# A routed expert layer whose weights are loaded once an expert, with the down products by Strassen's scheme

## The chip, the cores and the metric

The kernel is one program on one core of a Trainium2 chip. Its time is the device time of one execution in microseconds; the figure given is the median of three executions. The core has a matmul engine (PE, whose weight loads are listed apart as PEld), a vector engine (DVE), a scalar engine (ACT), a general engine (POOL), and a queue engine (SP) that starts transfers. Each of them takes its own instructions in order, and semaphores hold one behind another.

## The reference

Two layers over x of 2 x 2048 x 256, all in float32. Layer 0 is a gated linear attention and a quantised product; layer 1 is a 16-head attention with ALiBi bias and, beside it, a mixture of eight experts. Only the last is touched by the change:

```python
# xf: 4096 x 256; W_gate, W_up: 8 x 1024 x 256; W_down: 8 x 256 x 1024; TOP_K = 2
logits = xf @ gate_W.T
pi = _sinkhorn(-logits)                       # 20 rounds
_, top_idx = jax.lax.top_k(pi, TOP_K)
g = jnp.einsum('nd,efd->enf', xf, W_gate)
u = jnp.einsum('nd,efd->enf', xf, W_up)
y = jnp.einsum('enf,edf->end', jax.nn.silu(g) * u, W_down)
out = jnp.zeros_like(xf)
for k in range(TOP_K):
    out = out + y[top_idx[:, k], n_ar] * pi[:, k:k + 1]
```

Each token goes to two of eight experts, so there are 8192 rows in all. The routing worked out from the reference's inputs gives the experts 1047, 977, 950, 1003, 1054, 1044, 1029 and 1088 rows.

## The kernel before

The program runs layer 0, then the attention of layer 1 in "units" (one pass of the loop in `attention`: score matmuls L1823, exponentials L1832, weighted sums L1846), and in the gaps of those units the routing on DVE. The routing writes each row's token number and weights into a table in DRAM by 64 scatters (`sends`, L2222). When the units end, `Experts.run` (L2582) goes through the experts' rows.

**Blocks.** Rows are cut into full blocks of 256 (`BS`) and small ones of 32. An expert with `count` rows has `(count + 127) >> 8` full blocks; what is left goes into small blocks, four of which make a `Group`. The usual way handles 32 full blocks (`FULLS`) and two groups. The flags `c.special`, `c.more` and `c.general` say whether more blocks, or the whole general way (`general_way`, which computes everything again by other means), must be run after it.

**One block.** `load` gathers the expert's gate and up weights (2 MB, `load_gate_up`) by an indirect transfer from POOL (L2255), and reads the block's 256 table rows on SP (`load_places`, L2271); `load_down` gathers the down weights (1 MB) likewise; `fetch_rows` gathers the 256 tokens. `combine(u)` forms the sums of weights that Strassen's scheme (in Winograd's form: 7 products in place of 8) needs, four DVE operations of 128 x 512 for each half u of the hidden features; it overwrites the up weights with one of them. `open_rows` transposes the tokens on PE and forms their sums.

**The hidden products.** `hidden` (L2329) makes, for each u, seven products of four 128 x 128 x 128 matmuls. Their results go to three PSUM banks w, z and v, and ACT and DVE take partial results out between them. The order is h1 (to w), h2 (z), h6 (w), h5 (v), h7 (w), h4 (w), h3 (v). The last DVE operation of a half is `two *= sg[:, 1]`, behind the last SiLU.

**The down products.** `add_rows` (L2371) is a generator that `hidden` of the next block steps through by `next(others)`: once after h2, once after h5 and twice after h7, in each u, so eight times a block. Each step makes two matmuls of 128 x 128 x 256 (`multiply`); there are sixteen for a block, plain, into one bank `y_ps` with both row tiles side by side. At the end two DVE operations of 128 x 256 scale the sums (`send`, L2402) and two indirect transfers add them to the output. The last block's are made `apart`, each tile in a bank of its own.

`InOrder` keeps the expert phase's PE, DVE and ACT instructions in the order in which the program states them. So the place of a DVE operation in the program is its place in DVE's queue. PE takes matmuls in order too. In the traces one float32 matmul is two records.

**The order of one pass of the loop** in `run` is: `load` of block n+2; the generator of block n-1's down products; `hidden` of block n with, inside it, `combine(1)` of block n (u = 0, after the first step of the generator) and `combine(0)` of block n+1 (u = 1), `fetch_rows` of n+2 and `open_rows` of n+1; then `load_down` of n+2, and a step of a group if one is due.

Of the kernel before, what the change touches and what calls it, by code (L numbers as in the profile page):

```python
# [64 lines left out]
P = 128  # L65
# [3 lines left out]
ST = 512  # L69
# [23 lines left out]
NBLK = NFULL + NSMALL  # L93
ROWS = NFULL * BS + NSMALL * SB
FULLS, GROUPS = 2 * B * N // BS, 2
SPARE = B * N
RW = NE + 1
SINKHORN_ITERS = 20
# [1604 lines left out]
def attention(  # L1703
# [41 lines left out]
    def decide():  # L1745
        yield from routing.blocks(p2)

        high = p2.tile([P, 1], F32, tag="high", name="high")
        vector.tensor_reduce(high, norms[:, 0, :], AX.X, ALU.max)
        small = p2.tile([P, 1], F32, tag="small", name="small")  # L1750
        inside = p2.tile([P, NSTRIP * HG * 8], F32, tag="sk_part", name="inside", bufs=1)
        vector.tensor_scalar(
            inside, spans.rearrange("p s h n j -> p (s h n j)"), math.exp(-SPAN), None, ALU.is_ge
        )
        vector.tensor_reduce(small, inside, AX.X, ALU.min)
        yield
        least = p2.tile([P, 1], F32, tag="least", name="least")
        entry = p2.tile([P, NT, NE], F32, tag="sk_ex", name="entry")
        vector.tensor_tensor(entry, routing.second, pi, ALU.mult)
        yield  # L1760
        of_token = p2.tile([P, NT], F32, tag="sk_r", name="of_token")
        vector.tensor_reduce(of_token, entry, AX.X, ALU.max)
        vector.tensor_reduce(least, of_token, AX.X, ALU.min)
        yield
        within = p2.tile([P, 1], F32, tag="within", name="within")
        vector.tensor_scalar(within, least, TINY, None, ALU.is_ge)
        vector.tensor_tensor(within, within, small, ALU.mult)
        vector.tensor_scalar(least, grown, GROWTH, None, ALU.is_le)
        vector.tensor_tensor(within, within, least, ALU.mult)
        yield  # L1770
        yield
        ps = ps_m.tile([1, P + 1], F32, tag="mm", name="d_ps")
        nc.tensor.matmul(ps[:, 0:P], lhsT=high, rhs=ident, start=True, stop=True)
        nc.tensor.matmul(
            ps[:, P : P + 1], lhsT=within, rhs=c.ones_mat[:, 0:1], start=True, stop=True
        )
        yield
        row = p2.tile([1, P + 1], F32, tag="drow", name="drow")
        vector.tensor_copy(row, ps)
        both = p2.tile([1, P // 2], F32, tag="dboth", name="dboth")  # L1780
        vector.tensor_tensor(both, row[:, 0 : P // 2], row[:, P // 2 : P], ALU.mult)
        vector.tensor_scalar(both, both, 0.98 * LIMIT**2, None, ALU.is_le)
        ok = p2.tile([1, 1], F32, tag="dok", name="dok")
        vector.tensor_reduce(ok, both, AX.X, ALU.min)
        vector.tensor_scalar(row[:, P : P + 1], row[:, P : P + 1], float(P), None, ALU.is_equal)
        vector.tensor_tensor(ok, ok, row[:, P : P + 1], ALU.mult)
        vector.tensor_scalar(ok, ok, -1.0, 1.0, ALU.mult, ALU.add)
        vector.tensor_copy(c.general, ok)
        vector.tensor_tensor(ok, ok, routing.over[:, 0:1], ALU.max)
        vector.tensor_copy(c.special, ok)  # L1790
        yield
# [101 lines left out]
    def rooms(name, n, shape, dt=F32):  # L1893
# [8 lines left out]
        if name == "group_s":  # L1902
            return p2.tile(shape, F32, tag="sk_equal", name=name, bufs=1)
        if name == "wgateup":
            return operands.heads[(0, 1, 3)[n % 3]].rearrange("p j t -> p (j t)")
        if name == "wdown" and n % 3 < 2:
            return operands.heads[2][:, n % 3, :]
        if name in ("hT", "wdown"):
            room = large("pt", 2 if name == "wdown" else n % 2)
            return room if name == "wdown" else room.rearrange("p (f r) -> p f r", f=NFC)  # L1910
        early = operands.first_values.rearrange("p t d -> p (t d)")
        late = other_values.rearrange("p t d -> p (t d)")
        rest = partial(large, "pt", 3)
# [25 lines left out]
        return p2.tile(shape, dt, tag=name, name=name, bufs=5)  # L1939

    bias = value_bias()
    experts = Experts(tc, a, out, c, rooms, range(FULLS), range(GROUPS))
    ahead = experts.todo[0:2]
    for n, (pieces, widths, masks, ended) in enumerate(units):
        if n in (len(units) // 4 - 4, len(units) // 4):
            next(bias)
        if n == len(units) - BEGIN:
            for left in (background, decision, sends):
                for _ in left:
                    pass  # L1950
            for block in ahead:
                block.load_places()
            for block in ahead:
                block.load_gate_up()
        if n == len(units) - FETCH:
            for block in ahead:
                block.fetch_rows()
        if len(units) - FETCH < n <= len(units) - FETCH + 4:
            ahead[0].combine(0, range(n - len(units) + FETCH - 1, n - len(units) + FETCH))
        pt = scores(pieces, widths)  # L1960
        calm = not unmasked or len(unmasked[1]) <= CALM
        if unmasked:
            keep_only(*unmasked)
        unmasked = pt, masks
        before = len(chores)
        waiting.append((pieces, pt, ended))
        if len(waiting) > LATE:
            add_up()
        if before and chores:
            do_chore()  # L1970
        if routed:
            for _ in range(1 + n % 2):
                next(sends, None)
            if calm:
                next(decision, None)
        elif calm:
            routed = next(background, True) is True
        if n == len(units) - 4:
            ahead[0].open_rows()
    keep_only(*unmasked)  # L1980
    while waiting:
        add_up()
    for block in ahead:
        block.load_down()

    def rest():
        while chores:
# [6 lines left out]
class Routing:  # L1994
# [3 lines left out]
    def __init__(self, tc, vector, pool, a, c, group):  # L1998
# [15 lines left out]
        self.first, self.second = (  # L2014
            pool.tile([P, NT, NE], F32, tag=name, name=name) for name in ("first", "second")
        )
        self.over = pool.tile([1, 2], F32, tag="over", name="over")
        self.places = [
            pool.tile([P, NT], I32, tag=name, name=name) for name in ("place0", "place1")
        ]  # L2020
# [5 lines left out]
    def steps(self, pool, psum, pi):  # L2026
# [119 lines left out]
        for to, mark in zip(self.places, (first, second)):  # L2146
# [4 lines left out]

            vector.tensor_scalar(to, at, float(ROWS - 1), None, ALU.min)
            yield
        self.end = end

    def blocks(self, pool):

# [43 lines left out]
        for n in range(2):  # L2201
# [3 lines left out]
            )  # L2205
            vector.tensor_copy(self.c.wpart[:, n, :], part)
        over = self.over
        for n, done in enumerate((FULLS, 4 * GROUPS)):
            vector.tensor_scalar(
                over[:, n : n + 1], end[0:1, n, NE - 1 :], float(done), None, ALU.is_gt  # L2210
            )
# [31 lines left out]
class Block:  # L2243
# [156 lines left out]
    def send(self, c, ps, y, group=None):  # L2400
        e = self.e
        e.nc.vector.scalar_tensor_tensor(  # L2402
            y[:, c, :], ps, self.wt[:, c : c + 1], e.c.half_bias, ALU.mult, ALU.add
        )
        send = e.nc.gpsimd.indirect_dma_start(  # L2405
            out=e.out, in_=y[:, c, :], in_offset=None,
            out_offset=bass.IndirectOffsetOnAxis(ap=self.to[:, c : c + 1], axis=0),
            compute_op=ALU.add,
        ).ins


        if group and c:
            e.tc.declare_no_dep(send, group=group, reason="no row is in two of a block's tiles")
        if group:
            e.tc.add_to_no_dep_group(group, send)
            if e.latest:
                e.tc.add_manual_dep(
                    send, e.latest,
                    mybir.DependencyInfo(mybir.DependencyClass.Sync, mybir.DependencyReason.DATA),
                    reason="the same row may be in another block",  # L2420
                )
        else:
            e.latest = send.name


class Group:
# [121 lines left out]
class Experts:  # L2548

    def __init__(self, tc, a, out, c, rooms, blocks, groups):
        self.tc, self.nc, self.a, self.out, self.c = tc, tc.nc, a, out, c
# [1 line left out]
            InOrder(tc, engine) for engine in (self.nc.tensor, self.nc.vector, self.nc.scalar)  # L2555
        )
        self.rooms, self.latest = rooms, None
        self.todo = [Block(self, n, b) for n, b in enumerate(blocks)]
        self.between = deque()
        at = 3  # L2560
        for g in groups:
# [20 lines left out]
    def run(self, begun=None):  # L2582
# [12 lines left out]
        for n, block in enumerate(todo):  # L2595
            if n + 2 < len(todo):
                todo[n + 2].load()
            last = n + 1 == len(todo)
            others = todo[n - 1].add_rows() if n else begun or iter(())
            if last:  # L2600
                others = self.closing(others, block)
            meanwhile = (
                partial(block.combine, 1), (lambda: None) if last else partial(todo[n + 1].combine, 0)
            )
            for part, _ in enumerate(block.hidden(others, meanwhile)):
                if part == 1 and n + 2 < len(todo):
                    todo[n + 2].fetch_rows()
                if part == 2 and not last:
                    todo[n + 1].open_rows()
            for _ in others:  # L2610
                pass
            if n + 2 < len(todo):
                todo[n + 2].load_down()
            while between and between[0][0] <= n and not last:
                between.popleft()[1]()
        for _, step in between:
            step()

    def closing(self, others, block):

        while next(others, others) is None:
            next(others, None)
            yield
        yield from block.add_rows(apart=True)


def layer1_experts(tc, a, out, c, blocks, groups):
# [181 lines left out]
```

## Time and profile before

| what | value |
|---|---|
| median of three executions | 1504.07 us (1503.86 to 1504.57) |
| the profiled execution's own time | 1507.06 us |
| its span, first to last instruction | 1504.8 us |
| PE busy | 1444.7 us (96%) |
| DVE busy | 1009.7 us (67%) |
| ACT busy | 730.3 us (49%) |
| POOL busy | 538.4 us (36%) |
| moved by transfers | 191.94 MB |
| first hidden product of block 0 | 827.72 us from the span's start |
| last DVE scaling of the last block | begins at 1492.46 us |

In a timeline line the columns are: start, duration, engine, source line, operation, what it writes and reads, shapes, count, and in brackets how long the engine was idle before it and on whom it waited. Line L121 is the helper that keeps the order, so most operations of the expert phase carry it; the tile names tell them apart. Rooms are shared with attention, so `qk` holds weights there, `larger` and `va` hold hidden values and results. `h_ps` are the hidden banks, `y_ps` the down bank, `x_ps` the transposes of tokens, `o_ps` the attention's sums and `o_sb` their copies. A "wait" row gives an engine's total time behind another.

### The profile page before, as it was taken

The numbers are of one execution on the slowest core, as the hardware profiler recorded it, in microseconds if no ns is written. First come the engines' busy times: TensorE is split into PE (matmuls) and PEld (weight loads), VectorE is DVE, ScalarE is ACT, GpSimd is POOL, SyncE is SP. The second block draws the span as 40 slices with busy tenths as digits, with TensorE's granted clock in tenths as the row PEclk, the third lists the DMA queues.
The fourth block names the chain that finished last, engine by engine and source line by source line (L and its number), as shares of the span: only waits on it lengthen the run. The fifth ranks groups of instructions, "written<-read, shape, count | busy, mean of one in ns | idle before, by whom it ended". The sixth has DMA issues, their size and how long they took to land.

```text
span 1504.8 us, 33474 instructions
## 1 busy us (share of the span) xinstructions
PE 1444.7 (96%) x13712; PEld 1180.6 (78%) x13712; DVE 1009.7 (67%) x2567; ACT 730.3 (49%) x1557; POOL 538.4 (36%) x449
## 2 busy tenths in 40 slices
PE   7879999999989999999999999999999999999996
PEld 4656767676757777777666899989899998989995
DVE  6788677565448888874445767667666776666663
ACT  4444554555367888888876332333232332323231
POOL 4342222121120000399961234343434544343432
PEclk9999999999989999999999999999999999999998
DMA  8001010410353120420034656575766867576531
GB/s 236 0 15 59 30 57 30 120 58 29 81 151 60 31 62 25 95 35 5 5 131 157 224 195 199 191 286 175 261 198 218 252 210 254 193 253 241 174 83 23
DMA packets 75986, 191.94 MB, mean 128 GB/s; under 512 B 19136, under 2 KB 56768, under 8 KB 63360
## 3 DMA queue, kind: packets, MB, share of 16 engines
q0 software_dynamic: 28256, 144.23, 28.8%
q1 hardware_dynamic: 46464, 44.30, 11.9%
q8 instruction: 110, 1.80, 0.5%
q10 hardware_dynamic: 1104, 1.18, 0.3%
q14 instruction: 52, 0.43, 0.1%
HBM read 157.95 MB, written 32.10 MB: 126 GB/s over the span
## 4 chain that ended last, share of the span: by engine, by line
PE 56%; DVE 2%; ACT 1%; issue 1%; POOL 0%; POOLq 0%; another core or an unknown queue 0%
PE h_ps L121 26%; PE y_ps L121 15%; PE sc L1823 6%; PE o_ps L1846 5%; PE f_ps L1544 1%; PE h_ps L2491 1%; PE x_ps L121 1%; DVE pt L121 1%; ACT pt L1832 1%; PE h_ps L2526 0%; DVE o_sb L121 0%; ACT larger L121 0%; DVE onT L121 0%; DVE on L121 0%; DVE larger L121 0%
## 5 line engine op out<-in xcount | busy, mean ns | idle before, releaser
L1832 ACT ACTIVATE pt<-sc 128x512 f32<-128x512 f32 (+5 forms) x746 | 312.4, 517 | 78.2 <-issue 39.2
L1823 PE MATMUL sc<-qk 32*128 32x256 f32 (+3 forms) x3022 | 208.1, 361 | 3.6 <-ACT pt L1832 1.6
L121 DVE TENSOR_TENSOR larger<-larger,h_ps 128x512 f32<-128x512 f32 x160 | 109.9, 687 | 144.3 <-ACT larger L121 79.0
L1823 PEld LDWEIGHTS sc<-qk 32*128 32x128 f32 x3022 | 158.9, 189 | 46.1 <-ACT pt L1832 25.3
L121 PE MATMUL y_ps<-qk,larger 128*128 128x256 f32 x704 | 173.4, 380 | 0.3 <-DVE larger L121 0.3
L1846 PE MATMUL o_ps<-pt,va 128*32 128x256 f32 (+3 forms) x3022 | 166.2, 341 | 3.2 <-DVE o_sb L121 1.9
L121 ACT COPY larger<-h_ps 128x512 f32<-128x512 f32 x128 | 74.5, 582 | 172.7 <-PE h_ps L121 168.2
L121 DVE TENSOR_TENSOR pt<-pt,keepmask 128x128 f32<-128x128 f32 x512 | 117.4, 283 | 48.0 <-ACT pt L1832 46.9
L2405 POOL DMA_INDIRECT out<-va,to x64 | 102.7, 1604 | 124.3 <-DVE larger L121 49.1
L1846 PEld LDWEIGHTS o_ps<-pt,va 128*32 128x32 f32 x3022 | 103.3, 111 | 51.0 <-issue 20.8
L2222 POOL DMA_INDIRECT table<-rows,place x64 | 68.2, 1066 | 194.1 <-DVE pt L121 181.7
L121 PEld LDWEIGHTS y_ps<-qk,larger 128*128 128x128 f32 x704 | 123.9, 191 | 12.3 <-DVE larger L121 0.7
L121 PEld LDWEIGHTS h_ps<-va,qk 128*128 128x128 f32 x1024 | 126.6, 192 | 7.6 <-ACT larger L121 2.3
L121 PE MATMUL h_ps<-va,qk 128*128 128x128 f32 x1024 | 130.6, 276 | 1.9 <-ACT larger L121 1.9
L2568 POOL DMA_INDIRECT xb<-normed,to x64 | 65.5, 1024 | 140.5 <-DVE by L2291 71.8
L121 ACT ACTIVATE larger<-larger 128x512 f32<-128x512 f32 x64 | 40.4, 632 | 117.8 <-DVE larger L121 117.8
L121 ACT ACTIVATE va<-va 128x512 f32<-128x512 f32 x64 | 40.4, 632 | 100.2 <-DVE va L121 96.3
L121 PE MATMUL y_ps<-larger 128*128 128x256 f32 x320 | 79.0, 380 | 0.0
L121 POOL TENSOR_TENSOR pause<-ones_mat,expo 128x4 f32<-128x4 f32 x64 | 68.6, 1072 | 2.0
L121 ACT COPY va<-h_ps 128x512 f32<-128x512 f32 x64 | 36.9, 577 | 56.4 <-PE h_ps L121 51.1
L121 PE MATMUL h_ps<-larger,qk 128*128 128x128 f32 x512 | 62.7, 276 | 0.0
L121 PEld LDWEIGHTS h_ps<-larger,qk 128*128 128x128 f32 x512 | 59.7, 192 | 2.1 <-issue 2.1
(318 smaller groups left out, 2798.5 us busy)
## 6 DMA issues: line engine op xcount, KB each, us to landing
qk<-qk SPq DMA_DIRECT2D x32, 256.0 KB
qk<-qk SPq DMA_DIRECT2D x64, 128.0 KB
va<-v SPq DMA_DIRECT2D x4, 1208.0 KB
v<-v SPq DMA_DIRECT2D x8, 574.0 KB
normed<-xn SPq DMA_DIRECT2D x8, 512.0 KB
out<-acc SPq DMA_DIRECT2D x16, 256.0 KB
acc<-in_x SPq DMA_DIRECT2D x7, 512.0 KB
table<-rows,place POOLq DMA_INDIRECT x64
```

Of the source, the lines that this page charges most:

```text
L121: return lambda *a, **k: self.tc.keep_in_program_order(begin(*a, **k))
L1544: multiply(out[r : r + HR], left[:, r : r + HR], *args, **how)
L1823: nc.tensor.matmul(scs[r][:, at : at + q1 - q0], lhsT=heads[rows, 1, kb * P : (kb + 1) * P], rhs=heads[rows, 0, qt * QT + q0 : qt * QT + q ...
L1832: nc.scalar.activation(pt[:, r, part], scs[r][:, part], AF.Exp)
L1846: nc.tensor.matmul(sums[bank][r * HR : (r + 1) * HR, to + q0 : to + q1], lhsT=values[b, way][:, kb, h * VC : h * VC + HR], rhs=pt[:, r, at ...
L2222: send = self.tc.keep_in_program_order(self.nc.gpsimd.indirect_dma_start(out=self.c.table, in_=self.rows[:, t, :], in_offset=None, out_off ...
L2405: send = e.nc.gpsimd.indirect_dma_start(out=e.out, in_=y[:, c, :], in_offset=None, out_offset=bass.IndirectOffsetOnAxis(ap=self.to[:, c : ...
L2491: self.e.nc.tensor.matmul(ps[rows, :], lhsT=self.xT[:, c * P + r * SB : c * P + (r + 1) * SB], rhs=self.w[:, r, at : at + ST], start=c == ...
L2568: self.nc.gpsimd.indirect_dma_start(out=to, out_offset=None, in_=self.c.normed, in_offset=bass.IndirectOffsetOnAxis(ap=at, axis=0),)
```

## The change

The usual way now requires that each expert has exactly four full blocks (`OWN = FULLS // NE`): a third entry of `over` is 1 where that holds, and the flag for the general way is set where it doesn't. An `Expert` object loads its weights once by plain transfers on SP: gate and up in eight pieces of 256 KB (four for each u), down in one of 1 MB, two experts' worth of room each. `combine` runs once an expert. A new `turn_down` forms four sums of the down weights once an expert, and a new `sums` forms four sums of the hidden values once a block, behind `hidden`. `add_rows` makes seven products of four 128 x 128 x 128 matmuls in seven steps; their results lie in three quarters w, z, v of the one bank `y_ps`, and seven DVE operations of 128 x 128 (`put`) take them out. The last block's down products stay plain and apart.

```diff
+        vector.tensor_tensor(ok, ok, routing.over[:, 2:3], ALU.mult)
         vector.tensor_scalar(ok, ok, -1.0, 1.0, ALU.mult, ALU.add)
         vector.tensor_copy(c.general, ok)
...
+        own = tile_("own_blocks", [1, NE])
+        vector.tensor_scalar(own, self.full[0:1, :], float(OWN), None, ALU.is_equal)
+        vector.tensor_reduce(over[:, 2:3], own, AX.X, ALU.min)
...
         if name == "wgateup":
-            return operands.heads[(0, 1, 3)[n % 3]].rearrange("p j t -> p (j t)")
+            return operands.heads[n % 2].rearrange("p j t -> p (j t)")
+        if name == "wdown":
+            return operands.heads[2][:, n % 2, :]
...
-    experts = Experts(tc, a, out, c, rooms, range(FULLS), range(GROUPS))
+    experts = OwnExperts(tc, a, out, c, rooms, range(FULLS), range(GROUPS))
...
+        if n == len(units) - FETCH - 4:
             for block in ahead:
                 block.load_places()
-            for block in ahead:
-                block.load_gate_up()
+        if 0 <= n - len(units) + BEGIN < 8:
+            u, part = divmod(n - len(units) + BEGIN, 4)
+            experts.experts[0].load_gate_up(u, range(part, part + 1))
...
-    for block in ahead:
-        block.load_down()
+    experts.experts[0].load_down()
...
+class Expert:
+    def load_gate_up(self, u, parts=range(4)):
+        if not u:
+            self.w = self.e.rooms("wgateup", self.k, [P, 4 * FF])
+            self.wgu = self.w.rearrange("p (j c f) -> p j c f", j=2, c=2)
+        rows = self.e.a["wgateup"][self.k * P : (self.k + 1) * P, :]
+        for n in parts:
+            at = slice(n * FF + u * ST, n * FF + (u + 1) * ST)
+            self.e.tc.keep_in_program_order(
+                self.e.nc.sync.dma_start(out=self.w[:, at], in_=rows[:, at])
+            )
...
+    def turn_down(self):
...
+        vector.tensor_tensor(t1, b12, b11, ALU.subtract)
+        vector.tensor_tensor(t2, b22, t1, ALU.subtract)
+        vector.tensor_tensor(t3, b22, b12, ALU.subtract)
+        vector.tensor_tensor(t4, b21, t2, ALU.subtract)
+        self.parts = (b11, b21, b22, t4, t1, t2, t3)
...
+class OwnBlock(Block):
...
+    def sums(self):
...
+        vector.tensor_tensor(s1, a21, a22, ALU.add)
+        vector.tensor_tensor(s2, s1, a11, ALU.subtract)
+        vector.tensor_tensor(s3, a11, a21, ALU.subtract)
+        vector.tensor_tensor(s4, a12, s2, ALU.subtract)
+        self.parts = (a11, a12, s4, a22, s1, s2, s3)
+
+    def add_rows(self, apart=False):
+        if apart:
+            yield from super().add_rows(True)
+            return
+        e = self.e
+        y = e.rooms("y", self.n, [P, NC, E])
+        ps = e.rooms("y_ps", self.n, [P, ST])
+        w, z, v = (ps[:, n * P : (n + 1) * P] for n in range(3))
...
+        def product(n, to, first=False, last=False):
+            for f in range(4):
+                e.tensor.matmul(
+                    to, lhsT=self.parts[n - 1][:, f, :], rhs=self.expert.parts[n - 1][:, f, :],
+                    start=first and f == 0, stop=last and f == 3, skip_group_check=True,
+                )
+
+        def put(c, half, src, more):
+            e.vector.scalar_tensor_tensor(
+                y[:, c, half], src, self.wt[:, c : c + 1], more[:, half], ALU.mult, ALU.add
+            )
...
+        product(1, w, first=True)
+        put(0, left, w, bias)
+        yield
+        product(2, z, last=True)
+        put(0, left, z, y[:, 0, :])
+        yield
+        product(6, w)
+        put(0, right, w, bias)
+        yield
+        product(5, v)
+        yield
+        product(7, w)
+        put(1, right, w, bias)
+        put(1, right, v, y[:, 1, :])
+        yield
+        product(4, w, last=True)
+        put(1, left, w, bias)
+        self.scatter(1, y)
+        yield
+        product(3, v, last=True)
+        put(0, right, v, y[:, 0, :])
+        self.scatter(0, y)
+        yield
...
+class OwnExperts(Experts):
+    def bring(self, n):
+        k, part = divmod(n, OWN)
+        if k + 1 < NE and part < 2:
+            self.experts[k + 1].load_gate_up(part)
+        elif k + 1 < NE and part == 2:
+            self.experts[k + 1].load_down()
+
+    def meanwhile(self, n):
+        k, part = divmod(n, OWN)
+        first, second = [], []
+        if part == 0:
+            first.append(partial(self.experts[k].combine, 1))
+        if n == 0:
+            second.append(self.experts[0].turn_down)
+        if part + 1 == OWN and k + 1 < NE:
+            first.append(self.experts[k + 1].turn_down)
+            second.append(partial(self.experts[k + 1].combine, 0))
+        return [lambda steps=steps: [step() for step in steps] for steps in (first, second)]
+
+    def behind(self, n):
+        if n + 1 < len(self.todo):
+            self.todo[n].sums()
```

## The prediction

> **What bounds the kernel now.** First the waits of PE's two rows from 845 to 1480 us, the experts' phase:
>
> ```profile
> engine line waited for: us in total, times, longest us
> PEld h_ps L2491 <- issue: 7.2, 24, 0.3
> PEld h_ps L121 <- issue: 4.2, 6, 0.8
> PEld h_ps L121 <- ACT larger L121: 0.2, 1, 0.2
> ```
>
> In 635 us PE waits 0.2 us for another engine. So the phase lasts as long as its matmuls, and any wait put on PE comes in full. The timeline gives a block's order and prices:
>
> ```profile
> 862.17 1.07 DVE L121 TENSOR_TENSOR va<-va 128x256 f32<-128x256 f32 x3
> 863.15 0.87 DVE L2402 SCALAR_TENSOR_TENSOR va<-y_ps,wt,half_bias 128x256 f32<-128x256 f32 x2
> 864.70 1.95 PE L121 MATMUL h_ps<-va,qk 128*128 128x128 f32 x16
> 864.90 0.69 DVE L121 TENSOR_TENSOR va<-va,h_ps 128x512 f32<-128x512 f32 x1 [0.21 <-PE h_ps L121]
> 865.62 0.63 ACT L121 ACTIVATE va<-va 128x512 f32<-128x512 f32 x1 [3.60 <-DVE va L121]
> 866.28 0.69 DVE L121 TENSOR_TENSOR larger<-larger,va 128x512 f32<-128x512 f32 x1 [0.69 <-ACT va L121]
> ...
> 867.49 0.68 DVE L121 TENSOR_TENSOR larger<-qk 128x512 f32<-128x512 f32 x1
> 868.21 0.69 DVE L121 TENSOR_TENSOR qk<-qk 128x512 f32<-128x512 f32 x1
> 868.82 0.68 DVE L121 TENSOR_TENSOR larger<-larger,qk 128x512 f32<-128x512 f32 x1
> 869.54 0.69 DVE L121 TENSOR_TENSOR larger<-qk,larger 128x512 f32<-128x512 f32 x1
> 870.89 1.89 PE L121 MATMUL y_ps<-qk,larger 128*128 128x256 f32 x8
> 872.62 1.05 PE L121 MATMUL h_ps<-va,qk 128*128 128x128 f32 x8
> 874.40 1.95 PE L121 MATMUL h_ps<-va,qk 128*128 128x128 f32 x16
> 876.19 1.03 PE L121 MATMUL y_ps<-qk,larger 128*128 128x256 f32 x4
> 884.55 1.95 PE L121 MATMUL h_ps<-larger,qk 128*128 128x128 f32 x16
> ```
>
> A block begins at 864.70 and the next at 884.55: 19.85 us. Starts give the pace. Eight y records take 872.62 - 870.89 = 1.73, so 0.216 each; sixteen h records take 876.19 - 874.40 = 1.79, so 0.112 each. A float32 matmul is two records. Note also where the last DVE operation of the old block lies: at 866.28, 1.58 us into the new one.
>
> Then the end of attention, for one question: what does PE wait for when DVE reads one half of a PSUM bank and PE writes the other?
>
> ```profile
> 820.78 0.41 DVE L121 STREAM_TRANSPOSE o_sb<-o_ps 128x256 f32<-128x256 f32 x1
> 821.24 0.85 PE L1846 MATMUL o_ps<-pt,va 128*32 128x256 f32 x15 [0.94 <-DVE o_sb L121]
> 822.12 0.45 DVE L121 STREAM_TRANSPOSE o_sb<-o_ps 128x256 f32<-128x256 f32 x1
> 822.60 0.25 DVE L121 RECIPROCAL inv<-o_sb 128x16 f32<-128x16 f32 x1
> ```
>
> A step's two groups lie in the two halves of one bank. The read at 820.78 is of group 0 (no reciprocal follows it), the one at 822.12 of group 1 (one does). The matmuls between them fill group 1's half, and yet they start 0.05 us after group 0's read ends. The wait is by bank, not by column.
>
> **The change part by part.** *Down products.* Before: 16 matmuls x 2 x 0.216 = 6.92 us a block. After: 28 x 2 x 0.112 = 6.25. Halving the width doesn't quite halve the time, so 0.67 is saved, not an eighth of 6.92 (0.86). Blocks 1 to 31 each carry such a set: 31 x 0.67 = 20.8 us off the path.
>
> *The down bank's waits.* w, z and v share one bank, and each `put` stands in the program ahead of the next product. By the row at 821.24, product 2 waits for product 1's `put`, 6 for 2's, 5 for 6's, 4 for 7's two, 3 for 4's. What it costs depends on how early DVE gets there. A block from its start, with the rows' durations:
> PE: h1, h2, product 1, h6, h5 at 0.89 each, so product 2 is due at 4.46.
> DVE: `two *=` ends at 2.28 (866.28 + 0.69). The new `sums`, four of 128 x 512, stand next: two of them wait for the one before, as in the weights' sums at 867.49 to 870.23, so 2.6; they end at 4.88. Then the addition of h2, 4.80 to 5.49, and only then the first `put`. Its price: 0.476 for 128 x 256 (the pair at 863.15: 0.87 with overlap) less 128 elements at 1.04 ns is 0.34; it ends at 5.75. Product 2 starts at 5.81: **1.35 us of wait**.
> Product 6 follows h7 and starts at 7.69 without a wait. Its `put` stands behind `two + v`, which waits for ACT's copy of h7: 8.57 to 9.26, so the `put` ends at 9.52 and product 5, due at 8.59, starts at 9.58: **0.99 of wait**. Each restart costs PE 0.10, as eight records took 0.99 after a wait at 842.96 where 0.89 is usual. In u = 1 products 7, 4 and 3 come after h2, h5 and h7, so a hidden product or two lie between each `put` and its successor; no wait. So a plain block takes 19.85 + 2.54 - 0.67 = 21.7.
> In the first and last block of an expert DVE also has four weight sums (2.6) between the first `put` and the second. Product 6 then waits 0.9, and product 5 still 0.6: 3.2 in all.
> Sum: 16 plain blocks x 2.54 = 40.6; 14 others (blocks 3, 4, 7, 8 to 28) x 3.2 = 44.8; block 31 steps through the generator in pairs, so products follow their predecessor's `put` directly: 6. The groups' matmuls (3.6 us for gate, up and down, about 1 for their transposes) stand ahead of a block's h1 at eight places and let DVE catch up: by the same laying-out three blocks that begin an expert get back 2.2 each, three plain ones 1.45, the two behind transposes 1.0: -12.8. Total +78.6.
> Bounds: 0 if waits go by column, 78.6 by bank. I take the bank. [...] Column guards, tempting by the code's disjoint quarters, would give -20.8 plus some 5 of late DVE in the 14 blocks: 1489. [...]
>
> *DVE's load.* Gone: eight weight sums a block and two sendings (0.87). Come: four hidden sums, seven `put`s (about 2), and 12 weight sums per expert, three a block. At 0.69 that is 5.5 + 0.87 against 2.7 + 2 + 2.1: equal. DVE doesn't become the bound; its order does the harm.
>
> *Transfers.* POOL loses 64 gathers of 0.94 us; nothing on PE waited for them. 24 MB of block weights move in place of 96, on SP, behind the table load of n+2. They wait there for weights two experts old, which are free. A half's 1 MB at the 250 GB/s of this phase takes about 4 us, against two to three blocks until `combine`: nothing, and 4 us for each of seven experts if that cover went. Expert 0's down weights are due at `turn_down` in block 0, some 840 us (the sums at 840.02 stand there now); gathers into that room went at 819.22, SP is free by 826.87, so they land near 833. If late, DVE and block 0 wait a few us, once. Scatters: two a block as before, on a freer POOL.
>
> *The ends of attention.* The table loads move 17 units later on SP; now the queue stands at them for 127.1 us (SP's waits, longest "<- DMA table"), for the scatters, over at 775.7. Unit -15 is near 779 and the rows are used at 788.95: nothing; if later, DVE waits. The eight early loads have 15 units or more (over 30 us) before their first sum. Two gathers of 2 MB at 778.54 and 779.79 go, and there the scores crawl: 784.37 - 775.20 = 9.2 us for two units that take 2.2 to 2.4 elsewhere, with waits put down to "issue". Bounds 0 and -4.7; I take -3, since the groups' gathers at 775.98 stay. The guard's four small DVE operations (0.16 each by the cast at 788.95) hide in attention's idle DVE.
>
> Together: -20.8 + 78.6 - 3 = +55. The profiled execution took 1507.06 (span 1504.8), 3.0 above the median of the runs; the sum is a difference, so I set it on the median: 1504 + 55 = **1559**.
>
> **The rivals.** *Guards by column* (other side): the step is product 2's start. For it: nothing in the code shares a column. Against: the row at 821.24. It gives 1489, less 3: 1486. The turn is at 0.67 us of wait a block; with less the change is faster. Chance 0.06.
> *Half the wait*: the hidden sums don't stand ahead of the first `put`, or DVE runs closer than laid out. Then product 2 starts near 4.5 and only product 5 waits, 1.1 a block: 31 x 0.43 - 3 = +10, 1514. Against: `InOrder` states the order. Chance 0.05: 0.02 slower, 0.02 the same, 0.01 faster.
> *The guard sends it the general way*: the whole calculation again, over 1000 us more. Against: `full` is (count + 127) >> 8, which is 4 for 897 to 1152 rows, and all eight counts lie between 950 and 1088. Chance 0.01.
> *As worked out*, 0.88.
>
> **How the numbers follow.** Half a microsecond a block either way is 15 us, the eight relieved blocks and the -3 another 7: 1535 to 1575 for the likeliest case, and with 0.12 outside its mechanism the range stays there. Under 0.2% (3 us, about what a measurement can tell from no change): faster 0.07, same 0.02, slower 0.91.
>
> **What would show it.** PE rows of y_ps x8 with "<-DVE va" before them, about two a block, 1.3 and 1.0 us; blocks of 21.7 us; `sums` on DVE 2.3 us into a block; the y records at 0.112; POOL's gathers of weights gone; traffic down by some 75 MB. Wrong if y_ps matmuls start while a `put` runs, or if PE's waits in the phase are under 20 us.

## The result, and the profile after

The changed kernel takes 1569.52 us (median of four, 1567.17 to 1570.72) against 1504.32 for the kernel before on the same chip: a ratio of 1.0427, 95% interval 1.0409 to 1.0445. It is slower by 65 us, where 55 were forecast (1559, in a range of 1535 to 1575). In a second set of runs, on chip 15, the ratio was 1.0419 (1.0392 to 1.0447).

From the page of the changed kernel: PE's busy time, the chain that ended last by engine, the costliest row of the down products (busy, mean ns | idle before, releaser), and what was read from memory.

```profile
PE 1446.8 (92%) x14456; PEld 1192.1 (76%) x14456; DVE 1022.1 (65%) x2689; ACT 732.3 (47%) x1557; POOL 466.6 (30%) x385
...
HBM read 82.45 MB, written 32.10 MB: 73 GB/s over the span
...
PE 39%; DVE 15%; ACT 3%; issue 3%; DMA 1%; POOL 0%; POOLq 0%; DVEq 0%; another core or an unknown queue 0%; ACTq 0%
...
L122 PE MATMUL y_ps<-qk,larger 128*128 128x128 f32 (+1 forms) x1768 | 245.4, 282 | 63.1 <-DVE va L122 62.6
```

PE is busy for 2 us more than before in a span that is 62.6 us longer, so the added time is idle time. The transfers did shrink, by 75 MB, and POOL by 72 us of work, but no end moved for it. The chain names the new limit: DVE rises from 2% to 15% of it, although its busy share fell from 67% to 65%.

PE's waits in the changed kernel's experts' phase (us in total, times, longest):

```profile
engine line waited for: us in total, times, longest us
PEld y_ps L122 <- DVE va L122: 77.5, 76, 3.2
PE y_ps L122 <- DVE va L122: 62.6, 71, 3.0
PEld h_ps L2627 <- issue: 7.5, 26, 0.3
```

Before, the first two rows did not exist. `va` is the output of the `put`s. (PE's own figure is smaller by the weight load that stands between the release and the first matmul: 192 ns in the mean of the 1768 loads for y_ps.) A plain block in the timeline of the changed kernel:

```profile
1022.64 1.95 PE L122 MATMUL h_ps<-larger,qk 128*128 128x128 f32 x16
...
1024.23 0.69 DVE L122 TENSOR_TENSOR larger<-larger,va 128x512 f32<-128x512 f32 x1 [0.70 <-ACT va L122]
1024.43 1.06 PE L122 MATMUL y_ps<-qk,larger 128*128 128x128 f32 x8
1024.96 2.62 DVE L122 TENSOR_TENSOR larger<-larger 128x512 f32<-128x512 f32 x4
1025.32 1.06 PE L122 MATMUL h_ps<-second,va 128*128 128x128 f32 x8
1026.22 1.06 PE L122 MATMUL h_ps<-first,va 128*128 128x128 f32 x8
...
1027.49 0.68 DVE L122 TENSOR_TENSOR larger<-larger,h_ps 128x512 f32<-128x512 f32 x1
1028.09 0.34 DVE L122 SCALAR_TENSOR_TENSOR va<-y_ps,wt,half_bias 128x128 f32<-128x128 f32 x1
...
1028.49 1.16 PE L122 MATMUL y_ps<-qk,larger 128*128 128x128 f32 x8 [1.21 <-DVE va L122]
...
1031.19 0.69 DVE L122 TENSOR_TENSOR larger<-larger,h_ps 128x512 f32<-128x512 f32 x1 [1.16 <-ACT larger L122]
1031.80 0.34 DVE L122 SCALAR_TENSOR_TENSOR va<-y_ps,wt,half_bias 128x128 f32<-128x128 f32 x1
...
1032.20 1.16 PE L122 MATMUL y_ps<-qk,larger 128*128 128x128 f32 x8 [0.77 <-DVE va L122]
```

Product 1 is done by 1025.5, but its `put` stands in DVE's queue behind `sums` (1024.96) and the addition of h2 (1027.49) and runs at 1028.09. Product 2, in another quarter of the same bank, starts at 1028.49, behind that `put`. Product 5 starts at 1032.20, behind the `put` of product 6.

### The profile page after: what moved, and what is told of

The parts are those of the page before. It is cut to its first block, busy times and chain, and to the rows that moved or that the text cites. A ratio compares the mean times of both kernels' runs of the same rounds, so it can differ in the third digit from the quotient of the medians.

```text
span 1567.4 us, 35154 instructions
## 1 busy us (share of the span) xinstructions
PE 1446.8 (92%) x14456; PEld 1192.1 (76%) x14456; DVE 1022.1 (65%) x2689; ACT 732.3 (47%) x1557; POOL 466.6 (30%) x385
## 4 chain that ended last, share of the span: by engine, by line
PE 39%; DVE 15%; ACT 3%; issue 3%; DMA 1%; POOL 0%; POOLq 0%; DVEq 0%; another core or an unknown queue 0%; ACTq 0%
PE h_ps L122 16%; PE y_ps L122 9%; DVE larger L122 8%; PE sc L1825 6%; PE o_ps L1848 5%; DVE va L122 3%; DVE qk L122 1%; ACT larger L122 1%; ACT va L122 1%; PE h_ps L2627 1%; PE f_ps L1545 1%; DMA out<-group_y,group_to 1%; DVE pt L122 1%; ACT pt L1834 1%; PE h_ps L2662 0%
## 5 line engine op out<-in xcount | busy, mean ns | idle before, releaser
L122 PE MATMUL y_ps<-qk,larger 128*128 128x128 f32 (+1 forms) x1768 | 245.4, 282 | 63.1 <-DVE va L122 62.6
L122 PEld LDWEIGHTS y_ps<-qk,larger 128*128 128x128 f32 x1768 | 216.5, 192 | 81.0 <-DVE va L122 77.5
L122 PEld LDWEIGHTS h_ps<-va,qk 128*128 128x128 f32 x1024 | 122.0, 192 | 4.7 <-ACT larger L122 2.5
L122 DVE TENSOR_TENSOR larger<-larger 128x512 f32<-128x512 f32 x156 | 102.5, 690 | 24.3 <-ACT larger L122 22.3
L122 DVE SCALAR_TENSOR_TENSOR va<-y_ps,wt,half_bias 128x128 f32<-128x128 f32 x124 | 42.9, 346 | 51.5 <-PE y_ps L122 50.9
L122 PE MATMUL h_ps<-larger,qk 128*128 128x128 f32 x512 | 62.7, 276 | 0.0
```

The costliest lines, as they stand in the source:

```text
L122: return lambda *a, **k: self.tc.keep_in_program_order(begin(*a, **k))
```

## The experiments

Below, "phase" is the time from the first hidden product to the end of the span in the profiled execution. It leaves attention out, which needs care here (see the hardware section). A "plain block" forms no weight sums; "weight blocks" (an expert's first and last) do. Block lengths are distances between the blocks' row fetches on DVE. The ratio compares medians of two to ten executions with the kernel before on the same chip, and attention is in it; a "repeated" kernel was run again, in another set.

| kernel | ratio to before, 95% interval | phase, us | plain block | weight blocks |
|---|---|---|---|---|
| before (profile / repeated) | 1 | 677.1 / 676.0 | 19.85 | 19.85 |
| changed (profile / repeated) | 1.0427 / 1.0419 | 742.7 / 743.2 | 21.71 | 22.39, 22.77 |
| two banks | 0.9936 (0.9914 to 0.9959) | 674.9 | 19.19 | 20.79, 20.92 |
| one bank, sums behind the put (profile / repeated) | 1.0386 / 1.0415 | 743.0 / 743.9 | 20.23 | 23.7, 24.1 |
| plain down products | 0.9921 (0.9900 to 0.9942) | 674.1 | 19.85 | 19.85 |
| one more sum | 1.0582 (1.0557 to 1.0607) | 774.4 | 22.43 or 23.7 | 23.1 to 24.1 |
| two banks, split weight sums | 0.9900 (0.9874 to 0.9926) | 662.9 | 19.19 | 19.60, 19.74 |
| the same, one more sum | 0.9985 (0.9970 to 1.0000) | 678.0 | 19.62 | 20.33, 20.9 |
| one bank, both moved and split | 1.0205 (1.0181 to 1.0230) | 714.6 | 20.23 | 21.62, 21.75 |
| two banks, both moved and split | 0.9865 (0.9844 to 0.9886) | 661.9 | 19.20 | 19.57, 19.70 |

**The bank.** The theory is that the waits come from w, z and v sharing a bank. The rival is that DVE is late as a whole, or that narrow products slow PE.

```diff
-        ps = e.rooms("y_ps", self.n, [P, ST])
-        w, z, v = (ps[:, n * P : (n + 1) * P] for n in range(3))
+        w = e.rooms("y_ps", 0, [P, ST])[:, 0:P]
+        ps = e.rooms("y_ps", 1, [P, ST])
+        z, v = ps[:, 0:P], ps[:, P : 2 * P]
...
-        product(2, z, last=True)
+        product(2, z, first=True, last=True)
```

> Theory (waits go by PSUM bank): w lies in one of the two down banks and z and v in the other, so product 2 no longer stands behind the first put, nor product 5 behind that of product 6. PE's waits for DVE before y_ps matmuls, 62.6 us in the changed kernel, fall under 10; a plain block takes about 19.2 us in place of 21.7; the time is about 1490 us (1484 to 1497), below the kernel before. Rival (the products wait because DVE as a whole is late, or because the narrow products slow PE down): the bank makes no difference, blocks stay near 21.7 and the time within 10 us of 1569.

Measured: 1492.11 us, ratio 0.9936, and a plain block of 19.19. The same operations in the same order on every engine, with only the place of the results changed, are worth 68 us of phase. The time lies in the expected range with help from elsewhere: attention ended 13 us earlier in this profile than in the changed kernel's (811.55 against 824.74). Against the kernel before, two banks save only 1 to 2 us of phase; the rest of the 8 us lies ahead of the phase. PE's waits with two banks, 845 to 1450 us:

```profile
engine line waited for: us in total, times, longest us
PEld y_ps L122 <- DVE va L122: 18.4, 13, 1.7
PE y_ps L122 <- DVE va L122: 15.9, 13, 1.5
```

That is 16 us, not the under 10 expected. What is left lies in the weight blocks, as the timeline of this kernel shows:

```profile
874.33 0.68 DVE L122 TENSOR_TENSOR qk<-qk,qk 128x512 f32<-128x512 f32 x1
874.94 0.34 DVE L122 SCALAR_TENSOR_TENSOR va<-y_ps,wt,va 128x128 f32<-128x128 f32 x1
875.20 0.68 DVE L122 TENSOR_TENSOR larger<-larger,h_ps 128x512 f32<-128x512 f32 x1
875.33 1.16 PE L122 MATMUL y_ps<-qk,larger 128*128 128x128 f32 x8 [1.33 <-DVE va L122]
```

The first line is the last of four weight sums. They stand ahead of product 2's `put` (874.94), and product 5 (875.33) shares that bank now.

**Where the hidden sums stand.** One bank as in the changed kernel; `sums` only names the tiles, and its four operations run behind the first `put`.

```diff
         product(1, w, first=True)
         put(0, left, w, bias)
+        self.form()        # the four operations of sums()
         yield
```

> One bank as in the changed kernel, but the four hidden sums stand behind the first put instead of ahead of the next block. Theory (product 2's wait is made by the bank together with the place of the sums): product 2 starts about 4.5 us into a block without a wait; product 5 still waits 0.9 us, since its wait is made by the addition of h7, not by the sums; plain blocks take 20.3 us, blocks with weight sums stay near 22.4, since there product 6 now waits for both sets of sums. Time about 1547 us (1540 to 1555). Rival (the load of DVE, not its order): the same work lies on DVE, so 1569.

Measured: 1557.11 us, ratio 1.0386. The plain block is as expected, 20.23, with one wait of 0.77 at product 5: the sums' place made product 2's wait, the addition of h7 makes product 5's. But the time missed the range by 2 us, although attention ended 12 us earlier than in the changed kernel's profile, and the phase gained nothing: the weight blocks take 23.7 and 24.1 where 22.4 was expected. The reason is below, under "A wait that costs twice".

**The loads alone.** No sums, no `turn_down`, and the down products plain:

```diff
-        if apart:
-            yield from super().add_rows(True)
-            return
+        yield from super().add_rows(apart)
+        return
```

> The loads once an expert by plain transfers alone: the down products are made as in the kernel before (16 of 256 columns, no hidden sums, no sums of down weights). Theory (loads and weight sums once an expert cost the experts' phase nothing, and end attention 3 us earlier): 1501 us (1499 to 1504), blocks of 19.85. Rival (the loads on SP, or the eight weight sums that now stand together, delay blocks): over 1506, with waits in the first blocks of experts.

Measured: 1488.14 us, ratio 0.9921. Blocks of 19.85 us and no wait of PE for another engine: loading and summing weights once an expert is neutral in the phase (674.1 against 676.0). Most of the 12 us by which it beats the kernel before cannot lie there; it lies ahead of the phase, where attention ends earlier on this chip than the theory's 3 us (last section).

**A dose.** The last of the hidden sums is made twice.

```diff
         vector.tensor_tensor(s4, a12, s2, ALU.subtract)
+        vector.tensor_tensor(s4, a12, s2, ALU.subtract)
```

> One more DVE operation of 128 x 512 at the end of the hidden sums (the last one is made twice). Theory (the sums stand on PE's path by way of the first put): 0.65 us for nearly each of 31 blocks, 16 to 20 us, 1585 to 1590. Rival (the loss lies in the puts or in PE, and DVE at 65% has room): under 4 us more.

Measured: 1588.61 us. The undisturbed plain blocks show the price, 22.43 - 21.71 = 0.72: the operation is paid for in full, on an engine that is busy 65% of the time. The phase grew by more than 31 such operations, 774.4 - 742.7 = 31.7 us. Some plain blocks take 23.7: behind 14 of its waits the clock fell, as told under "A wait that costs twice". That the time still met the range is luck, since attention ended 10 us earlier here (814.86 against 824.74).

**The rest of the two-bank wait.** Weight sums in two pairs: two behind product 1's `put`, two behind product 2's (`turn_down` and `combine` are divided alike).

```diff
             next(others, None)
-            meanwhile[u]()
+            meanwhile[u](0)
...
             product(5, v, first=True)
             next(others, None)
+            meanwhile[u](1)
```

> Two down banks as before, and the sums of weights in two pairs: two behind product 1's put, two behind product 2's. Theory (what is left of the wait in the two-bank kernel is product 5, 1.33 us in the blocks that form weight sums, since the put of product 2 stands behind four sums): these waits go, such a block takes 19.3 in place of 20.8, the experts' phase falls from 675 us to 660, and the ratio to before is 0.985 (0.980 to 0.989). Rival (the sums are only moved, and the next wait, of the hidden product 3 for the addition of h7, takes the place of product 5's): blocks stay at 20.5 or more and the ratio at 0.993.

Measured: 1490.13 us, ratio 0.9900, phase 662.9. The interval reaches into the expected 0.980 to 0.989; the forecast middle was too low. Weight blocks went from 20.8 to 19.6. The rival's new wait, product 3 for h7's addition, is at most the 0.4 to 0.55 us that these blocks still take over a plain one.

**The dose again, with two banks.**

> The kernel with two banks and split sums, with the last hidden sum made twice, as was done with one bank, where it cost some 20 us. Theory (the operation costs only by way of the put that the next product waits for): 0 to 4 us more than without it, since no product follows its predecessor's put into the same bank. Rival (DVE's total load is the bound): some 20 us more here too.

Measured: 1503.51 us, ratio 0.9985: about 13 us more (15 by the phase), not 0 to 4 and not 20. Both theories missed. The plain block grows by 0.43 (19.19 to 19.62), a weight block by 0.7 or more, with y_ps waits behind `va` again (13.5 us in all). The expectation overlooked a pair: product 6 still writes w's bank, and product 1's `put` stands behind the sums. In the kernel without the dose that `put` is about 0.3 us early (the dose of 0.73 less the 0.43 that a block grew by). So the place in the queue costs here too; two banks had only moved it just out of reach.

**Both kernels again, for profiles on one chip.**

> The kernel before, unchanged, for a profile on the same chip as the others of this set. Two theories on the end of attention, where the changed kernel's first hidden product came 3 us earlier: if the two gathers of 2 MB that ran there slowed the scores, the crawl of the scores between 775 and 790 us shows here too and the first product comes near 828; if the granted TensorE clock made it (it was 0.74 and 0.61 in two stretches of the crawl), the first product comes 10 us or more earlier wherever the clock stays at 1.00 there. In both the experts' phase lasts 677 us from the first hidden product to the end.

> The changed kernel, unchanged, on the same chip. The experts' phase lasts 743 us from the first hidden product to the end as in its first profile, with 62 us of PE's waits for DVE at y_ps; the ratio to before is 1.04 again. The first hidden product comes near 812 if the granted clock sets it, as in the four kernels of the first set, near 825 otherwise.

Measured: 1504.80 and 1568.74 us. Phases 676.0 and 743.2, and 62.7 us of waits: the loss reproduces. First hidden products at 827.05 and 822.64. The crawl of the scores shows in the kernel before while the clock stands at 1.00 (PE busy for 2.30 of the 4 us from 778), so the clock alone doesn't make it.

**A wait that costs twice.** The kernel with the sums behind the put was run again. Its timeline in a weight block, and then PE's windows across it (length, busy time, records, granted clock, DMA share, GB/s):

> The kernel with the four hidden sums behind the first put, one bank, once more, beside the next two. PE's waits in blocks that form weight sums are 2.2 to 2.3 us long, and in the first run the granted clock fell behind most of them, eight records taking 2.08 us in place of 1.06. If that belongs to the length of the wait it shows again here, at 12 or more of these blocks, and the experts' phase lasts 740 us again.

```profile
1268.06 0.69 DVE L122 TENSOR_TENSOR larger<-qk,larger 128x512 f32<-128x512 f32 x1
1268.67 0.34 DVE L122 SCALAR_TENSOR_TENSOR va<-y_ps,wt,va 128x128 f32<-128x128 f32 x1
...
1269.07 1.34 PE L122 MATMUL y_ps<-qk,larger 128*128 128x128 f32 x8 [2.32 <-DVE va L122]
1270.45 0.35 DVE L122 SCALAR_TENSOR_TENSOR va<-y_ps,wt,half_bias 128x128 f32<-128x128 f32 x1 [0.85 <-PE y_ps L122]
1270.86 2.08 PE L122 MATMUL y_ps<-qk,larger 128*128 128x128 f32 x8 [0.44 <-DVE va L122]
1272.72 1.34 PE L122 MATMUL h_ps<-va,qk 128*128 128x128 f32 x8
```

```profile
1263.07:1266.49 3.42, 3.42 (x33) 1.00 0.33 38
1266.49:1269.90 3.41, 1.09 (x10) 1.00 0.00 0
1269.90:1273.31 3.41, 2.97 (x14) 0.50 0.00 0
1273.31:1276.73 3.42, 3.42 (x33) 1.00 0.00 0
```

PE waits 2.32 us, restarts at full speed, and then the clock is granted at half for 3.4 us (the row at 1269.90): eight records take 2.08 in place of 1.06. This followed 12 of the 14 waits of 2.19 to 2.34 us in each of the two runs, and 14 of 21 waits of 1.94 us or more in the run with the dose. Measured: 1559.97 us, phase 743.9. The next kernel splits the weight sums as above, so that the same wait comes in two pieces:

> One bank, the hidden sums behind the first put as in the kernel beside it, and the sums of weights in two pairs, one behind the first put and one behind the second. The waits of a block that forms weight sums are about as long in sum (2.7 us) but come in two pieces of 1.3 to 1.4. Theory (a wait of 2 us or more lowers TensorE's granted clock for the next 2 to 3 us, and that took back what the moved sums had given): no y_ps or h_ps records at half speed behind waits, the clock at 1.00 from 850 to 1500, such blocks 22.1 us in place of 23.7 to 24.1, the experts' phase about 715 us (705 to 722). Rival (the blocks are long because of the waits themselves): blocks near 23.7 and a phase of 740.

```profile
1251.02 0.34 DVE L122 SCALAR_TENSOR_TENSOR va<-y_ps,wt,va 128x128 f32<-128x128 f32 x1
...
1251.42 1.16 PE L122 MATMUL y_ps<-qk,larger 128*128 128x128 f32 x8 [0.99 <-DVE va L122]
...
1253.61 1.16 PE L122 MATMUL y_ps<-qk,larger 128*128 128x128 f32 x8 [1.03 <-DVE va L122]
1254.60 1.06 PE L122 MATMUL h_ps<-va,qk 128*128 128x128 f32 x8
```

Measured: 1528.57 us, ratio 1.0205, phase 714.6. The pieces are about 1.0 us, shorter than the 1.3 to 1.4 expected, and the records behind them keep 1.06. Two of the fourteen weight blocks did show slow records behind such a pair (23.37 in place of 21.7, and 27.14 in place of 25.5), so the theory's "none" is too strong, and "2 us or more" is not what the runs show; the last section has their counts. Weight blocks fell by 2.1 to 2.4 us. The wait shown fell by 2.32 + 0.44 - 0.99 - 1.03 = 0.74 of that in one, and the slow records in the fence before it make about 1.5 (2.08 and 1.34 where 1.06 is usual, and 1.34 where a start behind a wait takes 1.16).

**Everything together.** Two banks, the weight sums in pairs, the hidden sums behind the first `put`.

> Two down banks, weight sums in two pairs, and the hidden sums behind the first put instead of ahead of the block. In the kernel without the last step what is left is 6.7 us of short waits in 15 places, so there is little to gain: a phase of 656 to 664 us against 662.9, a ratio to before of 0.985 to 0.991. If the sums there hold up product 5 by way of the second put in the blocks with weight sums, it is no better or up to 6 us worse.

Measured: 1477.43 us, ratio 0.9865, phase 661.9, faster than both kernels (14 of the 21 us against the kernel before are phase). Only 0.8 us of PE's waits for `va` at y_ps is left from 845 to 1450, after 1.6 without this step. The last step itself gained nothing that can be told from the kernel without it.

## Why the prediction held, and what was mis-sized

*PE as the bound, and the price of a product.* Held. Down products in seven narrow steps save 19.85 - 19.19 = 0.66 a block once their waits are gone; 0.67 was worked out.

*The wait goes by bank.* Held: product 2 starts 5.85 us into the block above (forecast 5.81), product 5 at 9.56 (9.58), a plain block takes 21.71 (21.7). With two banks these waits vanish from plain blocks (19.19 us). What makes a product wait is the kernel's guard, which follows the bank; what the hardware would do without it was not tried.

*DVE's order and not its load.* Held. Without moving any work off DVE the phase went from 743 to 662.

*The rivals.* "Guards by column" gave blocks without waits; that is what two banks brought, not what the change did. "Half the wait" is the plain block of the kernel with the sums behind the put, 20.23.

*The sizes.* By the profiled executions the phase grew by 742.7 - 677.1 = 65.6 us; the steps gave 78.6 - 20.8 = 57.8. Four terms account for the 7.8, each against the blocks of the kernel with plain down products at the same place:

- The groups' relief, put at 12.8, was 7.0. Eight places gave back 9.4 (0.7 to 1.8 each), but at two places a group took 1.2: its row fetch on DVE stands behind `sums` and ahead of the first `put`. In the timeline of the changed kernel:

```profile
932.55 2.62 DVE L122 TENSOR_TENSOR larger<-larger 128x512 f32<-128x512 f32 x4
...
935.10 0.14 DVE L2597 CAST group_to<-group_at 128x1 int32<-128x1 f32 x1
935.16 0.16 DVE L2598 COPY group_to<-nowhere 128x4 int32<-128x4 int32 x1
935.35 0.62 DVE L2600 CAST group_to<-group_at 32x1 int32<-32x1 f32 x4
...
936.87 0.34 DVE L122 SCALAR_TENSOR_TENSOR va<-y_ps,wt,half_bias 128x128 f32<-128x128 f32 x1
...
937.27 1.16 PE L122 MATMUL y_ps<-qk,larger 128*128 128x128 f32 x8 [2.40 <-DVE va L122]
```

- Weight blocks: seven of them took 22.77 where 22.4 was worked out, 2.7 us more together; the other seven 22.39.
- The last block: 34.3 us to its last scaling where the kernel before took 27.2, so +7.1 for a forecast of 5.3. Its product 2 waits 3.00 us, and the clock falls behind that wait too: sixteen hidden records then take 1.92 + 1.85 us in place of 2.12. So 1.65 of the 1.8 is the clock, for which the forecast had no term.
- After that scaling the program ends 2.2 us sooner than before.

5.8 + 2.7 + 1.8 - 2.2 = 8.1. Small slips in the working change nothing: the rival's -20.8 + 5 from 1504 is 1488, not 1489; and 250 GB/s is what single slices of the page before show (252 and 254), while 206 were moved in the mean from 845 to 1480 us, so that 1 MB takes 5 us at that rate, by estimate, in place of 4. The `put`s' price was sized well: 0.34 in the timeline above. The profile before has this kind of operation (SCALAR_TENSOR_TENSOR) at both widths, 476 ns for 128 x 256 (L2402) and 341 ns for 128 x 128 (L863), which is 1.05 ns an element.

*Attention's end.* The first hidden product came 3.0 us earlier, as forecast, and 4.4 in the repeated pair. The traces place the gain where the forecast did, at the two gathers of 2 MB; that these alone made it was not tested. In the repeated pair, ten of attention's exponentials (the 670th to the 680th, counted from 0) take 8.1 us in the kernel before and 4.5 in the changed one. PE there, first the kernel before (gathers issued at 777.43 and 778.68), then the changed one at the same work:

```profile
777.86 0.59 PE L1846 MATMUL o_ps<-pt,va 128*32 128x256 f32 x3
779.34 0.62 PE L1846 MATMUL o_ps<-pt,va 128*32 128x128 f32 x3 [0.89 <-issue]
780.78 1.03 PE L1846 MATMUL o_ps<-pt,va 128*32 128x256 f32 x16 [0.81 <-issue]
```

```profile
776.66 1.08 PE L1848 MATMUL o_ps<-pt,va 128*32 128x256 f32 x22
```

Why PE stands idle there stays open: by these rows it waits for nothing that the profile shows ("issue").

*The base.* The sum was set on the median 1504. The medians differ by 65.2, the two spans by 62.6: the profiled execution before was 3 us above its median.

## What to carry to other kernels

When results of successive matmul groups share a PSUM bank and the program guards by bank, each group is chained to the read of the one before: in this phase PE waited 62.6 us for such reads with one bank and 15.9 (845 to 1450 us) with two. The price was set by what stood ahead of that read in its engine's queue, not by how busy that engine was (DVE, 65%). Place such results in banks by the order in which they are read, and put long operations behind the read and not ahead of it: both together took the phase from 743 us to 662. With PE as the bound an added wait came in full: one more sum made an undisturbed plain block 0.72 us longer (22.43 against 21.71). And a wait could cost twice: the clock fell to half behind 12 of the 14 waits of 2.19 to 2.34 us, for 3.41 us in the block shown, which by estimate is up to 1.7 us of work (1.5 and 1.65 us are worked out above).

## What the runs showed of the hardware

*The clock fell by windows, not by single waits.* In the experts' phase of these profiles each stretch at half clock lasts 3.41 or 6.83 us (the one behind the last matmul apart), and within a profile the stretches begin whole multiples of 3.413 us apart. The rows under "A wait that costs twice" are cut by these windows: the wait of 2.32 us lies in one of them, and half clock fills the next. The wait of 2.40 us in the changed kernel, shown with the groups, falls across the end of a window, leaves PE busy for over 2 us in both, and goes unpunished:

```profile
932.45:935.87 3.42, 2.42 (x22) 1.00 0.56 89
935.87:939.28 3.41, 2.01 (x18) 1.00 0.13 38
```

The profiles have 2503 such windows at full clock from 845 us on. Half clock followed all 39 in which PE was busy for 1.40 us or less, 12 of the 15 between 1.40 and 1.75, and none of the 2449 above. So what a wait cost depended on where it fell. (In attention, where the matmuls use 32 rows, the fall came behind windows of 1.86 to 2.54 us and not behind one of 1.71: no single limit holds for both.)

*Attention's end differs between sets of runs, and the clock is the smaller part of it.* Windows of 40 us across the end of attention, first the kernel before, then the two-bank kernel (columns: PE, PEld, DVE, ACT, POOL, granted clock, DMA share, GB/s):

```profile
770.00:810.00 40.00, 37.53 (x520) 25.81 (x523) 17.68 (x59) 24.39 (x59) 12.99 (x13) 0.87 0.55 206
```

```profile
770.00:810.00 40.00, 38.86 (x710) 29.47 (x704) 27.66 (x100) 31.92 (x77) 9.10 (x10) 1.00 0.29 95
```

In the profiles from chips 3 and 7 the clock stayed at 1.00 here, and the first hidden product came at 809 to 815 us. In those from chip 15 and in the first pair the clock dipped (0.87 to 0.91, before and changed alike), and it came at 823 to 828. But the dip is two or three windows at half, so at most 3.4 or 5.1 us, and it follows a window at full clock in which PE was busy for only 1.9 to 2.5 of 3.4 us. The lag also begins earlier. From 640 to 780 us, first the changed kernel on chip 15, then the last kernel of the table on chip 7:

```profile
640.00:780.00 140.00, 138.45 (x2433) 101.30 (x2432) 73.28 (x272) 118.28 (x284) 121.54 (x115) 1.00 0.17 43
```

```profile
640.00:780.00 140.00, 140.00 (x2529) 104.27 (x2528) 78.43 (x287) 122.87 (x295) 124.03 (x118) 1.00 0.18 38
```

At a granted clock of 1.00 in both, the first has made 96 matmul records fewer, with the same attention code. Why is open, and so is whether the chip or the set of runs makes it. So the same code can differ by some 10 us ahead of the phase. The kernel before was not profiled on chips 3 and 7. An estimate from its median there (1499.95 and 1498.49, less the 2.2 us by which its times exceed its spans, less a phase of 676.5) puts its first hidden product near 821 and 820, so the earlier loads may be worth 6 to 12 us there, against 3.0 and 4.4 in the two pairs of profiles.
